# Rows of x held for 20 edge batches in place of 16, three selector buffers, skip pairs every eight batches

## The chip, the cores and the metric

The kernel runs on one core of one Trainium2 chip. The metric is the device time of one execution in microseconds (us); less is better. The engines are named as the profile names them: PE is the matrix engine (PEld its weight loads), DVE the vector engine, ACT the scalar engine, POOL the GpSimd engine, SP the engine that issues plain DMAs. POOL computes next to nothing here: it issues the indirect DMAs that gather rows by index.

## What is computed

One layer of a graph network over 12,500 nodes of 160 channels (64 scalars and 32 vectors of 3) and 400,000 edges that are sorted by destination. Cut to what matters:

```python
h = relu(layernorm(x))                       # per node, 160 channels
y = h @ W_l1 * a / sqrt(..)                  # per node: the scalars with one matrix, the vectors with another
s = h @ W_sc * a / sqrt(..)                  # per node: the skip part
w = silu(edge_attr_4 ... @ fc_W1) @ fc_W2    # per edge: 16 inputs -> 64 -> 192 weights
m = products of w, y[src] and 4 edge values  # per edge: 96 scalars and 96 vectors
z = zeros.at[dst].add(m)                     # sum over the edges of a destination
out = x + C_S * s + C_X * (z @ W_l2) * a     # per node
```

All of it is float32. The length embedding of an edge has 16 values, its attribute 4.

## The kernel before

**Node stage** (lines 393 to 520). The 12,500 nodes are 98 tiles of 128 rows; a step takes two tiles. Each step loads x into `acc`, which later becomes the output, takes mean and variance on DVE (`moments`, `center`), turns the rows on PE (`turn_rows`), maps them with the first weights (`map_rows`) and writes the result y to the DRAM tensor `y_d` (`leave`). The steps run as a software pipeline of eight stages, `q` counts them.

**Edge stage** (lines 537 to 866). The 400,000 edges are 3,125 tiles of 128, and four tiles make a batch: 782 batches, numbered `b`. For each batch

- POOL issues four gathers of 128 rows of y by source index (`gather`, L570), four batches ahead. The first of the four waits for the matmuls of `sums(b - 4)`, by a dependency that is written out by hand.
- PE makes the edge weights from the hidden layer (`weigh`, L603), ACT copies the edge values beside them (L525), and DVE makes a selector (`own` L617, `sel` L619) and the products of weights and rows (`pr`, L530 and L534).
- PE sums the products by destination (`sums`, L633): eight matrix instructions into a window of 32 destinations, held in PSUM. DVE turns a finished window (L639, L640).

A hidden layer for four batches is made every fourth batch: `hidden_pair` at the end of the pass in which `b % 4 == 0`: two matmuls (L583), each into a PSUM buffer of the name `px`, which ACT empties (L588). There are two `px` buffers, and everything small on PE takes them in turn: the hidden layer, the output map of a group (`linear`, L646, emptied by ACT L648), its placing (`add`, L658, emptied by DVE L669), the turning and mapping of the skip part and of the rows of x.

Four windows make a group. A window is 24 tiles wide at the start and gets narrower with the place in the sorted list: 24, 12, 8, 6, 4 and at last 3 tiles, so that a group is 24, 12, 8, 6, 4 or 3 batches. Widths change at batches 96, 192, 312, 408 and 624. `linear`, `add` and `accumulate` of a group run in the second and third batch of the next one.

Two kinds of work are spread over the edge stage.

- **Batches from x.** For XB = 16 batches (b = 19, 35, 51 and so on, every SB = 16th) no row of y is gathered in the edge stage. Their rows of x are fetched during the node stage, while POOL has little else to do (`x_fetch`, L348, four fetches for three steps), and kept in SBUF in `xr`. In the sixteen batches before each is used, its rows are normalized, turned and mapped on the spot: a one-hot matrix (`hot`, DVE L717 and L720; `hot_turn`, PE L728, ACT L730) and matmuls look up scale and mean of the source nodes (`look_up`, PE L740; `pick`, DVE L745 and L746), ACT subtracts the mean (`x_center`, L750), PE turns (`x_turn`, L755 and L756) and maps (`x_map`, L768 and L769).
- **Skip pairs.** The skip part s is made for two node tiles at a time, 49 pairs, one every SK = 10 batches, from batch SS = 16 * XB + 8 = 264 on. Counted from the start of a pair: rows of x are loaded (`skip_load`), centred on DVE in batch 4 (`skip_center`, L686), turned on PE in batch 5 (`skip_turn`, L693 and L694, emptied by ACT L696), mapped in batch 7 (`skip_map`, L703 and L704) and added to the output in the same batch on DVE (`skip_add`, L712).

The order of all instructions on an engine is the order in which the program writes them (`manual_schedule`); the pass of batch b writes `weigh(b + 2)`, `linear` or `add`, the skip and x work, `products(b + 1)`, the adding, `sums(b)`, `gather(b + 4)` and `hidden_pair`.

Of the kernel before, what the change touches and what calls it, by code (L numbers as in the profile page):

```python
# [28 lines left out]
GT = 4  # L29
# [10 lines left out]
EARLY = 8  # L40
SB = 16
LATE = 8
XB = 16
SK = 10
LO = D - P
EPS = 1e-5
C_S = math.sin(math.pi / 8.0)
# [4 lines left out]
def kernel(  # L52
# [36 lines left out]
    NB = (T + GT - 1) // GT  # L89
# [35 lines left out]
    ra, nm = look[:, 0, :], look[:, 1, :]  # L125
    xr = const.tile([P, XB, GT, D], F32, name="xr")
    xi = const.tile([P, XB, GT], I32, name="xi")
    xp = const.tile([P, XB, GT], F32, name="xp")
    xt = const.tile([P, XB, GT], F32, name="xt")
    mv = const.tile([P, NT, 2], F32, name="mv")  # L130
# [177 lines left out]
    def node_dma(g, n, dma):  # L308

        f = min(g + n, N // P) - g  # L310
        if f:
            dma(slice(g * P, (g + f) * P), slice(0, f), P)
        if f < n:
            dma(slice((g + f) * P, N), slice(f, f + 1), N - (g + f) * P)
# [4 lines left out]
    def by_tile(ap):  # L319
        n = ap.shape[0]  # L320
        return ap.rearrange("(t p) c -> p t c", p=min(P, n))
# [8 lines left out]
    def x_batch(u):  # L330

        return SB * (u + 1) + 3

    def x_index():
        t = x_batch(0) * GT
        nc.sync.dma_start(xi, src[:, t:t + XB * SB * GT].rearrange("p (u r) -> p u r", r=SB * GT)[:, :, 0:GT])

    def x_split():

        part = rp.tile([P, XB, GT], I32, name="part")  # L340
        nc.vector.tensor_scalar(part, xi, P - 1, None, ALU.bitwise_and)
# [55 lines left out]
    with (  # L397
        tc.tile_pool(name="ny", bufs=2) as ny,
        tc.tile_pool(name="ns", bufs=4) as ns,
        tc.tile_pool(name="nd", bufs=4) as nd,  # L400
        tc.tile_pool(name="nd_pt", bufs=2, space=PSUM) as nd_pt,
        tc.tile_pool(name="nd_po", bufs=3, space=PSUM) as nd_po,
        tc.tile_pool(name="nd_ph", bufs=2, space=PSUM) as nd_ph,
    ):
        yss, hs, pts, hTs, pos, mapped, sts = ({} for _ in range(7))
        steps = [(g, n, j, min(HN, n - j)) for g, n in groups for j in range(0, n, HN)]

        def moments(q):
            g, n, j, m = steps[q]
            sts[q] = ns.tile([P, HN, 6], F32, name="st")  # L410
            for k in range(m):
                nc.vector.bn_stats(sts[q][:, k, :], acc[:, g + j + k, :])

        def center(q):

            g, n, j, m = steps[q]
            st = sts.pop(q)
            h = nd.tile([P, HN, D], F32, name="h")
            for k in range(m):
                nc.vector.bn_aggr(mv[:, g + j + k, :], st[:, k, :])  # L420
            for k in range(m):
                t = g + j + k
                nc.vector.tensor_scalar(h[:, k, :], acc[:, t, :], mv[:, t, 0:1], 0.0, ALU.subtract, ALU.max)
            hs[q] = h

        def roots(q):
            g, n, j, m = steps[q]
            if j + m == n:
                nc.scalar.activation(ra[:, g:g + n], mv[:, g:g + n, 1], AF.Sqrt, bias=eps)

        def scales(q):

            g, n, j, m = steps[q]
            if j + m == n:
                nc.vector.reciprocal(ra[:, g:g + n], ra[:, g:g + n])
                nc.vector.tensor_mul(ra[:, g:g + n], ra[:, g:g + n], a_sb[:, g:g + n])

        def turn_rows(q):
            m, h = steps[q][3], hs.pop(q)
            pt = nd_pt.tile([P, 2, HN, P], F32, name="pt")  # L440
            for k in range(m):
                nc.tensor.transpose(pt[:, 0, k, :], h[:, k, 0:P], ident)
                nc.tensor.transpose(pt[:, 1, k, :], h[:, k, LO:D], ident)
            pts[q] = pt

        def out_of_psum(q):
            m, pt = steps[q][3], pts.pop(q)
            hT = nd.tile([P, 2, HN, P], F32, name="hT")
            nc.scalar.activation(hT[:, :, :m, :], pt[:, :, :m, :], AF.Copy)
            hTs[q] = hT  # L450

        def map_rows(q):
            m, hT = steps[q][3], hTs.pop(q)
            po = nd_po.tile([P, HN, D], F32, name="po")
            for k in range(m):
                nc.tensor.matmul(po[:, k, 0:M0], hT[:, 0, k, :], wy0, start=True, stop=True)
                mapped[q] = nc.tensor.matmul(po[:, k, M0:], hT[:, 1, k, :], wy1, start=True, stop=True).ins.name  # L457
            pos[q] = po

        def leave(q):  # L460

            g, n, j, m = steps[q]
            if j == 0:
                yss[g] = ny.tile([P, GN, D], F32, name="ys")
            ys, po = yss[g], pos.pop(q)
            for k in range(m):
                nc.scalar.activation(ys[:, j + k, :], po[:, k, :], AF.Copy, scale=ra[:, g + j + k:g + j + k + 1])
            if j + m == n:
                node_dma(g, n, lambda rows, t, p: nc.sync.dma_start(by_tile(y_d[rows, :]), ys[:p, t, :]))
                del yss[g]  # L470


        LEAD = 5
        ready = ns.tile([P, 1], F32, name="ready")
        nc.scalar.activation(ready, eps, AF.Sqrt)
        node_weight_loads()
        edge_zeros()
        for i, (g, n) in enumerate(groups[:LEAD]):
            load_x(g, n)
            if i == 1:  # L480
                nc.sync.dma_start(a_sb, attr)
                x_index()
        last = len(steps) - 1
        more = list(groups[LEAD:])
        loads = edge_weight_loads()
        for q in range(len(steps) + 7):
            if q <= last and steps[q][2] == 0 and more:
                load_x(*more.pop(0))
            for f in range(4 * q // 3, 4 * (q + 1) // 3):
                if f < XB * GT:  # L490
                    x_fetch(f, mapped.get(q - 6))
            if q == 8:
                e4_load(0)
            for load in loads[2 * q - 24:2 * q - 22] if q >= 12 else []:
                load()
            if q == 24:
                for b in range(min(EARLY, NB)):
                    features(b)
            if q == 16:
                rows_of_windows()  # L500
                lowest(0)
            if q == 18:
                pt = nd_ph.tile([MW, P], F32, name="ph")[:windows_in(0), :]
                turn_low(0, pt)
                most(0, pt)
            if q == 22:
                spread(0, nd_ph.tile([P, MW], F32, name="ph")[:, :windows_in(0)])
            for stage, lag in ((scales, 3), (leave, 7), (out_of_psum, 4), (roots, 2), (turn_rows, 3), (map_rows, 5),
                               (moments, 0), (center, 1)):
                if 0 <= q - lag <= last:  # L510
                    stage(q - lag)
            if q == 2:
                node_weights()
            if q == last + 3:
                nc.vector.tensor_scalar(nm, mv[:, :, 0], -1.0, None, ALU.mult)
                x_split()
                edge_weights()
                relate(rp, 0)
        assert 12 + len(loads) // 2 <= last and 3 * XB * GT <= 4 * (last + 8) and x_batch(XB) <= NB
    before.close()  # L520


# [12 lines left out]
                                 wt[:, :n, 96 * x + M0:96 * (x + 1)].unsqueeze(2).to_broadcast([P, n, 3, M1]), y1)  # L535

    with (
        tc.tile_pool(name="selp", bufs=4) as selp,
        tc.tile_pool(name="prod", bufs=3) as prod,
        tc.tile_pool(name="xq", bufs=1) as xq,  # L540
        tc.tile_pool(name="sp", bufs=2) as sp,
# [131 lines left out]
        def skip_load(u):  # L673

            t, m = HN * u, min(HN, NT - HN * u)
            xs = sp.tile([P, HN, D], F32, name="xs")
            if t + m == NT and N % P:
                nc.vector.memset(xs[:, m - 1, :], 0.0)
            node_dma(t, m, lambda rows, k, p: nc.sync.dma_start(xs[:p, k, :], by_tile(x[rows, :])))
            xss[u] = xs, t, m  # L680
# [94 lines left out]
            nc.vector.tensor_tensor(part, part, vals[u][:, :, 0:1].to_broadcast([P, GT, 4]), ALU.mult)  # L775

        NU = (NT + HN - 1) // HN
        skips = {4: skip_center, 5: skip_turn, 7: skip_map, 8: lambda u: skip_load(u + 1) if u + 1 < NU else None}
        SS = SB * XB + 8
        xs_of = {x_batch(u) for u in range(XB)}  # L780

# [12 lines left out]
        for b in range(NB):  # L794
# [4 lines left out]
            q, r = divmod(b, KB)  # L799
# [4 lines left out]
            u, v = divmod(b, SB)  # L804
            su, sv = divmod(b - SS, SK)
            if b + 2 < NB:
# [28 lines left out]
                products(b + 1)  # L835
            if g and k == K - 1:
                accumulate(g - 1)
            if sv == 7 and 0 <= su < NU:
                skip_add(su)
            if picked is not None:  # L840
                pick(u, HN * (v == 6), *picked)
# [17 lines left out]
            if b % 4 == 0 and b + 4 < NB:  # L859
                hidden_pair((b + 4) // 2)  # L860
        assert SS + NU * SK <= first_of[GE] + K and NQ > 1
        for h in ([NG - 2] if NG > 1 else []) + [NG - 1]:
# [160 lines left out]
```

## Time and profile before

| | |
|---|---|
| three runs | 4700.06, 4708.81 and 4720.77 us, median 4708.81 |
| profiled execution | 4710.64 us, of which its instructions span 4708.8 |
| before the span's start and after its end | 1.8 us |
| first gather of y (end of the node stage) | at 115.6 us |
| first and last `own` (L617) of the 782 batches | 118.7 and 4694.6 us |
| busy: PE, DVE, POOL, ACT | 3891.7, 2736.7, 2968.3, 581.6 us |
| mean granted clock of PE | 0.906 of full |

How to read it: a group of instructions is given by its line, engine, operation and tiles, then the number of instructions, a bar, their busy time and the mean of one in ns, a second bar and the idle time of the engine just before them, with what ended most of that. A wait is put down to the engine whose semaphore came last. `remote` stands for a release that the profile can't name, `issue` for time in which the engine waited for nothing that it shows. Ends of matmuls are modelled. An indirect DMA on POOL is busy only while it is issued; its rows land later.

### The profile page before, as it was taken

The numbers are of one execution on the slowest core, as the hardware profiler recorded it, in microseconds if no ns is written. First come the engines' busy times: TensorE is split into PE (matmuls) and PEld (weight loads), VectorE is DVE, ScalarE is ACT, GpSimd is POOL, SyncE is SP. The second block draws the span as 40 slices with busy tenths as digits, with TensorE's granted clock in tenths as the row PEclk, the third lists the DMA queues.
The fourth block names the chain that finished last, engine by engine and source line by source line (L and its number), as shares of the span: only waits on it lengthen the run. The fifth ranks groups of instructions, "written<-read, shape, count | busy, mean of one in ns | idle before, by whom it ended". The sixth has DMA issues, their size and how long they took to land.

```text
span 4708.8 us, 46910 instructions
## 1 busy us (share of the span) xinstructions
PE 3891.7 (83%) x14078; PEld 2542.2 (54%) x14078; DVE 2736.7 (58%) x6877; ACT 581.6 (12%) x1845; POOL 2968.3 (63%) x3145
## 2 busy tenths in 40 slices
PE   7788888888788787887888888888888888888888
PEld 6455555555555455555555555555555555555555
DVE  5555555555555555555555656556556666666665
ACT  5111111111111101101110101111011111111100
POOL 5666666666666666666666666666666666666665
PEclk8889999999999998988888989998989998998889
DMA  7222222222222222222222222222222222222224
GB/s 192 69 63 65 66 66 65 66 67 64 60 64 67 66 69 67 67 66 67 70 68 62 65 63 67 66 68 63 63 66 65 68 64 63 65 64 67 59 62 117
DMA packets 262471, 328.58 MB, mean 70 GB/s; under 512 B 82888, under 2 KB 212216, under 8 KB 262216
## 3 DMA queue, kind: packets, MB, share of 16 engines
q0 software_dynamic: 150128, 256.23, 20.5%
q1 hardware_dynamic: 111590, 69.02, 5.2%
q8 instruction: 116, 1.90, 0.2%
q14 instruction: 139, 1.14, 0.1%
q10 hardware_dynamic: 498, 0.30, 0.0%
HBM read 307.67 MB, written 17.61 MB: 69 GB/s over the span
## 4 chain that ended last, share of the span: by engine, by line
PE 66%; another core or an unknown queue 15%; issue 7%; DVE 7%; ACT 2%; ACTq 1%; POOL 0%; DMA 0%; DVEq 0%; SPq 0%; POOLq 0%
PE pz L633 31%; PE pw L603 19%; PE px L646 6%; PE px L583 3%; DVE pr L534 2%; PE px L658 2%; DVE pr L530 1%; ACT hT L588 1%; ACTq L525 1%; DVE za L640 1%; DVE za L639 1%; PE po L457 1%; PE px L704 1%; POOL yg L570 0%
## 5 line engine op out<-in xcount | busy, mean ns | idle before, releaser
L570 POOL DMA_INDIRECT yg<-y_d,src_q x3061 | 2901.9, 948 | 1681.5 <-issue 795.2
L633 PE MATMUL pz<-pr,sel 128*128 128x320 f32 x6250 | 1950.3, 457 | 17.6 <-DVE za L640 15.2
L633 PEld LDWEIGHTS pz<-pr,sel 128*128 128x128 f32 x6250 | 1243.5, 204 | 542.6 <-issue 94.9
L603 PE MATMUL pw<-w,hT 128*128 128x384 f32 x3126 | 1233.8, 519 | 208.7 <-DVE pr L534 135.6
L603 PEld LDWEIGHTS pw<-w,hT 128*128 128x128 f32 x3126 | 590.3, 198 | 734.3 <-issue 375.5
L639 DVE STREAM_TRANSPOSE za<-pz 128x160 f32<-128x160 f32 x598 | 206.5, 345 | 1298.9 <-PE pz L633 551.3
L534 DVE TENSOR_TENSOR pr<-pw,yg 128x384 f32<-128x384 f32 x1532 | 773.5, 546 | 0.0
L530 DVE TENSOR_TENSOR pr<-pw,yg 128x512 f32<-128x512 f32 x766 | 523.2, 683 | 126.8 <-DMA yg<-y_d,src_q 118.3
L646 PE MATMUL px<-wo,za 128*128 128x160 f32 x1500 | 320.2, 376 | 294.4 <-ACT hT L588 198.2
L619 DVE TENSOR_TENSOR sel<-own,pw 128x512 f32<-128x512 f32 x782 | 536.9, 687 | 28.1 <-issue 1.2
L646 PEld LDWEIGHTS px<-wo,za 128*128 128x128 f32 x1500 | 290.2, 246 | 364.7 <-ACT hT L588 226.5
L525 ACT ACTIVATE pw<-ev 128x20 f32<-128x20 f32 x782 | 149.6, 191 | 2624.1 <-PE pw L603 970.4
L588 ACT ACTIVATE hT<-px 128x512 f32<-128x512 f32 x391 | 218.5, 595 | 968.9 <-remote 648.9
L583 PE MATMUL px<-xe,w 32*128 32x512 f32 x782 | 268.9, 658 | 66.2 <-ACT os L648 38.8
L617 DVE TENSOR_TENSOR own<-iota,pw 128x128 f32<-128x128 f32 x782 | 200.0, 256 | 177.1 <-ACT pw L525 133.8
L640 DVE STREAM_TRANSPOSE za<-pz 32x160 f32<-32x160 f32 x598 | 202.1, 338 | 20.5
L658 PE MATMUL px<-os,place 128*128 128x160 f32 x600 | 122.6, 332 | 79.0 <-ACT os L648 75.8
L669 DVE SCALAR_TENSOR_TENSOR acc<-px,a_sb,acc 128x160 f32 x300 | 113.9, 380 | 113.2 <-PE px L658 70.8
L658 PEld LDWEIGHTS px<-os,place 128*128 128x128 f32 x600 | 107.0, 211 | 131.8 <-ACT os L648 91.2
L583 PEld LDWEIGHTS px<-xe,w 32*128 32x128 f32 x782 | 70.9, 187 | 176.8 <-issue 95.7
L648 ACT ACTIVATE os<-px 128x160 f32<-128x160 f32 x150 | 45.3, 302 | 359.8 <-remote 168.4
L712 DVE SCALAR_TENSOR_TENSOR acc<-px,look,acc 128x160 f32<-128x160 f32 x98 | 32.9, 377 | 95.1 <-PE pz L633 39.7
(129 smaller groups left out, 1423.7 us busy)
## 6 DMA issues: line engine op xcount, KB each, us to landing
yg<-y_d,src_q POOLq DMA_INDIRECT x3061
xe<-in_e SPq DMA_DIRECT2D x784, 32.0 KB
xs<-in_x SPq DMA_DIRECT2D x48, 160.0 KB
acc<-in_x SPq DMA_DIRECT2D x11, 640.0 KB
y_d<-ys SPq DMA_DIRECT2D x11, 640.0 KB
out<-acc SPq DMA_DIRECT2D x11, 640.0 KB
raw<-in_e SPq DMA_DIRECT2D x32, 192.0 KB
src_q<-in_src SPq DMA_DIRECT2D x32, 48.0 KB
```

Of the source, the lines that this page charges most:

```text
L530: nc.vector.tensor_mul(pr[:, :n, :].rearrange("p t (x u) -> p t x u", x=2)[:, :, :, 0:M0], wt[:, :n, 0:NW].rearrange("p t (x u) -> p t x u ...
L534: nc.vector.tensor_mul(pr[:, :n, D * x + M0:D * (x + 1)].rearrange("p t (c u) -> p t c u", c=3), wt[:, :n, 96 * x + M0:96 * (x + 1)].unsqu ...
L570: fetch = nc.gpsimd.indirect_dma_start(out=yg[:, slot(t), :], out_offset=None, in_=y_d, in_offset=bass.IndirectOffsetOnAxis(ap=ev4[t // BL ...
L583: nc.tensor.matmul(ph, w1[r, :], xe[r, :], start=True, stop=True)
L588: nc.scalar.activation(hT, ph, AF.Silu, scale=1.0 / math.sqrt(FC_IN))
L603: nc.tensor.matmul(pw[:, 2 * k:2 * k + m, 0:NW], hT[:, o:o + P], w2[:, :m, :], start=True, stop=True)
L619: nc.vector.tensor_tensor(sel, own[:, :n, :].unsqueeze(2).to_broadcast([P, n, 4, WN]), wt[:, :n, NW:NW + 4].unsqueeze(3).to_broadcast([P, ...
L633: mm = nc.tensor.matmul(pz[:, 0:PC], sel[:, slot(t), :, :], pr[:, slot(t), :], start=o == 0, stop=last)
L639: nc.vector.transpose(zT[g][:, :, at_w], pz[:, D:PC].rearrange("p (k u) -> p k u", k=ZK))
L640: nc.vector.transpose(zT[g][0:32, :, at_w], pz[0:32, 0:D].rearrange("p (k u) -> p k u", k=ZK))
L646: nc.tensor.matmul(po[:m, :], za[:, k, :m], wo[:, k, :], start=k == 0, stop=k == ZK - 1)
L658: nc.tensor.matmul(ps[:, h, :], place[:m, h, :], os[:m, :], start=True, stop=True)
```

## The change

Three constants of the work spread over the edge stage change, and one pool.

- XB goes from 16 to 20. Twenty batches (b = 19 to 323) take their rows from x, so 64 fetches in the node stage become 80 and 3061 gathers become 3045. The fetches stand five to three node steps, and each still waits for the map of six steps before.
- The pool `selp`, which holds `own` and `sel`, has three buffers in place of four. `xr` grows by four times 4 x 160 floats for each partition.
- Skip pairs start at batch SS = 328 in place of 264, follow each other every 8 batches in place of 10, and centre, turn, map and load one batch earlier within a pair (3, 4, 6, 7 in place of 4, 5, 7, 8). The last of the 49 pairs begins at batch 712 in place of 744.

The diff:

```diff
-XB = 16
-SK = 10
+XB = 20
+SK = 8
...
-            for f in range(4 * q // 3, 4 * (q + 1) // 3):
+            for f in range(5 * q // 3, 5 * (q + 1) // 3):
                 if f < XB * GT:
                     x_fetch(f, mapped.get(q - 6))
...
-        tc.tile_pool(name="selp", bufs=4) as selp,
+        tc.tile_pool(name="selp", bufs=3) as selp,
...
-        skips = {4: skip_center, 5: skip_turn, 7: skip_map, 8: lambda u: skip_load(u + 1) if u + 1 < NU else None}
+        skips = {3: skip_center, 4: skip_turn, 6: skip_map, 7: lambda u: skip_load(u + 1) if u + 1 < NU else None}
...
-            if sv == 7 and 0 <= su < NU:
+            if sv == 6 and 0 <= su < NU:
                 skip_add(su)
```

Where a skip pair stands among the batches also changes. Since 264 and 328 are multiples of four, and 10 is not, a pair before was turned at b % 4 = 1 and mapped at 3, and the next one turned at 3 and mapped at 1, by turns. Now every pair is centred at b % 4 = 3, turned at 0 and mapped at 2.

PE's order around one skip pair of the stretch with windows of four tiles, before, from `sums(466)` on. L693 and L694 are the pair's turning, L646 and L658 `linear` and `add`, L583 the hidden layer, L178 and L187 small work on the next window starts:

```order
L633 MATMUL pz<-pr,sel 128x320 x4
L603 MATMUL pw<-w_94,hT 128x2x192 x2
L633 MATMUL pz<-pr,sel 128x320 x4
L583 MATMUL px<-xe,w_93 128x512 x2
L603 MATMUL pw<-w_94,hT 128x2x192 x2
L646 MATMUL px<-wo,za 128x160 x5
L693 MATMUL px<-ident,sh 128x128
L694 MATMUL px<-ident,sh 128x128
L693 MATMUL px<-ident,sh 128x128
L694 MATMUL px<-ident,sh 128x128
L187 MATMUL px<-ident,high 128x24
L633 MATMUL pz<-pr,sel 128x320 x4
```

The same place now, from `weigh(470)` on:

```order
L603 MATMUL pw<-w_94,hT 128x2x192 x2
L693 MATMUL px<-ident,sh 128x128
L694 MATMUL px<-ident,sh 128x128
L693 MATMUL px<-ident,sh 128x128
L694 MATMUL px<-ident,sh 128x128
L633 MATMUL pz<-pr,sel 128x320 x4
L583 MATMUL px<-xe,w_93 128x512 x2
L603 MATMUL pw<-w_94,hT 128x2x192 x2
L646 MATMUL px<-wo,za 128x160 x5
L187 MATMUL px<-ident,high 128x24
L633 MATMUL pz<-pr,sel 128x320 x4
```

The turning stood behind the hidden layer and behind `linear`; now it stands ahead of the sums and of the hidden layer, and takes a `px` buffer before the hidden layer takes both.

POOL's order, whole but for its start:

```order
 L262 MEMSET wor 128x800
 L264 MEMSET acc 128x160
-L348 DMA xr<-in_x,xi 128x160 x64
-L570 DMA yg<-y_d,src_q 128x160 x3061
+L348 DMA xr<-in_x,xi 128x160 x80
+L570 DMA yg<-y_d,src_q 128x160 x3045
 L876 TENSOR_LOAD far_i
```

Sixteen indirect DMAs move from the edge stage to the node stage, and nothing else of POOL's moves.

More of the change, by code (lines that the diff above doesn't have):

```diff
@@ L518 @@
                 relate(rp, 0)
-        assert 12 + len(loads) // 2 <= last and 3 * XB * GT <= 4 * (last + 8) and x_batch(XB) <= NB
+        assert 12 + len(loads) // 2 <= last and 3 * XB * GT <= 5 * (last + 8) and x_batch(XB) <= NB
     before.close()
```

## The prediction

> **What bounds the kernel now.** I read the page first, the engines' shares and the costliest groups.
>
> ```profile
> PE 3891.7 (83%) x14078; PEld 2542.2 (54%) x14078; DVE 2736.7 (58%) x6877; ACT 581.6 (12%) x1845; POOL 2968.3 (63%) x3145
> L570 POOL DMA_INDIRECT yg<-y_d,src_q x3061 | 2901.9, 948 | 1681.5 <-issue 795.2
> ```
>
> No engine is full. PE at 83% looks like the bound, but ends of matmuls are modelled and overlap. POOL is the one to look at: a gather is busy for 948 ns, yet the waits of POOL show a second cost that always comes with it.
>
> ```profile
> POOL yg L570 <- issue: 795.2, 2541, 4.6
> POOL yg L570 <- PE pz L633: 372.5, 149, 7.2
> POOL yg L570 <- remote: 314.1, 131, 3.7
> POOL yg L570 <- PE pw L603: 85.0, 66, 4.9
> ```
>
> 795.2 us over 2541 waits is 0.31 us each: the gap between two gathers in which POOL waits for nothing. So a gather takes 0.95 + 0.30 = 1.25 us of POOL, 3061 of them 3826 us, and four, a batch's worth, 5.0. The rest, 372.5 + 314.1 + 85.0 = 772 us in 346 waits, 2.2 us each, are stops in which POOL has used up its lead of four batches. The edge stage is thus POOL's queue plus its stops. The timeline shows what a stop is: POOL, then PE, then ACT in one of them, each row with start, duration and, in brackets, the idle time before it.
>
> ```profile
> 2511.18 0.94 POOL L570 DMA_INDIRECT yg<-y_d,src_q  x1 [0.30 <-issue]
> 2512.43 0.94 POOL L570 DMA_INDIRECT yg<-y_d,src_q  x1 [0.30 <-issue]
> 2515.77 0.94 POOL L570 DMA_INDIRECT yg<-y_d,src_q  x1 [2.39 <-remote]
> ...
> 2509.68 1.13 PE L583 MATMUL px<-xe,w 32*128 32x512 f32 x4
> 2511.64 1.56 PE L603 MATMUL pw<-w,hT 128*128 128x384 f32 x4 [0.84 <-DVE pr L534]
> 2516.22 1.80 PE L646 MATMUL px<-wo,za 128*128 128x160 f32 x10 [3.02 <-ACT hT L588]
> ...
> 2515.57 1.09 ACT L588 ACTIVATE hT<-px 128x512 f32<-128x512 f32 x2 [5.44 <-remote]
> ```
>
> The hidden pair fills both `px` buffers. The next user of `px`, here `linear`, needs one back and sits in PE's queue ahead of `sums(b + 1)`. ACT gets the hidden layer 4.8 us after PE's rows end (2509.68 + 1.13 against 2515.57), and POOL has run dry by then. So a small `px` user close behind, or ahead of, a hidden pair makes a stop.
>
> How long a batch takes by stretch is read from the rows of L617 (one for each batch) and of L570 in equal windows of time: four rows of the one, then three of the other. The first stretch is b = 192 to 267 (x batches), the second 268 to 311 (skip pairs; windows eight tiles wide in both), the third 624 to 753 (skip pairs, width 3), the last 754 to 780 (neither).
>
> ```profile
> 1176.10:1612.10 436.00, 19.76 (x76) 0.93 0.24 64
> 1612.10:1868.90 256.80, 11.58 (x44) 0.89 0.25 67
> 3740.30:4536.40 796.10, 32.25 (x130) 0.90 0.24 64
> 4536.40:4694.60 158.20, 6.66 (x27) 0.90 0.36 104
> ...
> 1176.10:1612.10 436.00, 273.81 (x289) 0.93 0.24 64
> 1612.10:1868.90 256.80, 165.95 (x176) 0.89 0.25 67
> 3740.30:4536.40 796.10, 493.26 (x521) 0.90 0.24 64
> ```
>
> A batch takes 5.74, 5.84, 6.12 and 5.86 us. Less 1.25 us for each gather, stops are 0.98 us a batch with x batches (436.0 - 361.3, over 76), 0.84 with skip pairs (256.8 - 220.0, over 44), 1.11 in the third.
>
> **The change part by part.** *Gathers.* Sixteen fewer in the edge stage: 16 x 1.25 = 20.0 us off POOL's queue.
>
> *The work that four x batches bring.* Their groups, with means of one:
>
> ```profile
> L740 PE MATMUL px<-look,sT 128*128 128x196 f32 x128 | 28.0, 344 | 2.4 <-ACT sT L730 2.1 <-issue 0.3
> L769 PE MATMUL px<-wy,sT 128*128 128x96 f32 x128 | 28.6, 308 | 0.0
> L768 PE MATMUL px<-wy,sT 128*128 128x64 f32 x128 | 24.4, 275 | 17.8 <-ACT hT L588 13.4 <-issue 4.4
> L755 PE MATMUL px<-ident,xr 128*128 128x128 f32 x64 | 20.0, 330 | 48.6 <-ACT hT L588 37.0 <-issue 8.5 <-ACT sT L758 3.0
> L756 PE MATMUL px<-ident,xr 128*128 128x128 f32 x64 | 19.4, 322 | 0.0
> L728 PE MATMUL px<-ident,oh 128*128 128x128 f32 x64 | 9.6, 273 | 0.0
> ```
>
> A sixteenth of the six is 8.1 us of busy PE, overlap taken off. DVE's and ACT's shares, a few us, lie beside engines that are 58% and 12% busy. What decides is not this but the stops: one `x_turn` and one `x_map` in sixteen batches stand at b % 4 = 1, right behind a hidden pair; 37.0 of L755's 48.6 us of idle time ended with ACT's hidden layer. From the stretches of equal width, x batches cost 0.98 - 0.84 = 0.14 us a batch more in stops if the skip pairs of the second stretch are free, 2.3 us for each x batch; and (0.14 + 0.27) x 16 = 6.6 if a skip pair costs what the last two stretches say (6.12 - 5.86 = 0.27 a batch, 2.7 a pair; an upper bound, since the last stretch is short and POOL runs out within it). Against 5.0 us saved, one x batch is worth between a gain of 2.7 and a loss of 1.6 us, four between -11 and +6. I take the middle, **-2 us**: the saving of 20 and a return of 18.
>
> *Skip pairs.* All 49 stay; none of them stands at b % 4 = 1 any more, where before each pair had one part, the turning or the mapping. That part came after `linear`, on the second `px` buffer, so it waited for the second hidden activation too (0.5 of the 1.09 us of L588 above), and its own 0.44 us (turning) or some 0.9 (mapping; below) stood before `sums(b + 1)` in the one pass of four that POOL waits for.
>
> ```profile
> 2503.44 0.27 PE L693 MATMUL px<-ident,sh 128*128 128x128 f32 x1
> 2503.99 2.32 PE L633 MATMUL pz<-pr,sel 128*128 128x320 f32 x8
> ...
> 2517.81 0.53 PE L703 MATMUL px<-ws,sT 128*128 128x64 f32 x2
> 2518.61 0.58 PE L703 MATMUL px<-ws,sT 128*128 128x64 f32 x2
> 2519.61 0.30 PE L187 MATMUL px<-ident,high 24*128 24x24 f32 x1
> ```
>
> The turning (L693, L694) runs from 2503.44 to 2503.88, the mapping, in the stretch above at half clock, from 2517.81 to 2519.61, so about 0.9 at full. Taken out of that pass, 0.5 + 0.65 = 1.15 us a pair, 56 us for 49, is the most. The least is nothing: 0.44 us is now ahead of `sums(b)` at b % 4 = 0, and 0.9 plus `skip_add` at 2, beside `add`. The cover there is POOL's lead, refilled by then; without it the 1.3 us a pair is back. I take a third, **-18 us**, because the stop itself stays wherever `linear` makes it: always in the 216 batches of width 4, which get 27 of the 49 pairs.
>
> *Selector buffers*: **0**. `sel(b + 1)` with three buffers waits for `sums(b - 2)`. It needs `weigh(b + 1)` anyway, and that stands behind `sums(b - 2)` in PE's order. If that cover were gone, `own` and `sel` (0.26 + 0.69 us) would come late.
>
> *Node stage.* Sixteen more fetches of 1.25 us are 20 us of POOL. POOL's rows there:
>
> ```profile
> 7.79 1.03 POOL L348 DMA_INDIRECT xr<-in_x,xi  x1 [1.76 <-DMA xi<-in_src]
> 102.99 0.95 POOL L348 DMA_INDIRECT xr<-in_x,xi  x1 [0.30 <-issue]
> 115.56 0.95 POOL L570 DMA_INDIRECT yg<-y_d,src_q  x1 [11.62 <-DMA xe<-in_e]
> ...
> 0.00:50.00 50.00, 33.72 (x217) 31.82 (x218) 28.64 (x154) 21.74 (x55) 32.63 (x49) 0.89 0.89 239
> ```
>
> 80 fetches without a pause end at 7.8 + 80 x 1.25 = 108, before the first gather, which waits for y and not for POOL. But the DMA engines are 89% busy in the first 50 us at 239 GB/s, and 16 fetches of 82 KB are 1.3 MB: 0 to 5.5 us. I take **+2**, because later they have room.
>
> *Sum*, against the profiled execution: 4710.6 - 20 + 18 - 18 + 0 + 2 = **4693 us**; the runs' median lies 1.8 below that execution.
>
> **The rivals.** *The turning blocks the hidden pair* (slower). The turning at b % 4 = 0 takes one `px` buffer; the first half of the hidden pair gets the other, and the second half must wait until ACT has copied the turning. The trace has this place with `linear` in it, where windows are three tiles wide:
>
> ```profile
> 3767.49 1.52 PE L646 MATMUL px<-wo,za 128*128 128x160 f32 x10
> 3768.85 2.32 PE L633 MATMUL pz<-pr,sel 128*128 128x320 f32 x8
> 3771.10 1.12 PE L583 MATMUL px<-xe,w 32*128 32x512 f32 x2
> 3776.48 2.07 PE L583 MATMUL px<-xe,w 32*128 32x512 f32 x2 [4.25 <-ACT os L648]
> ...
> 3776.12 0.30 ACT L648 ACTIVATE os<-px 128x160 f32<-128x160 f32 x1 [7.55 <-remote]
> ```
>
> The second half waited 4.25 us, for an ACT copy that began 7.1 us after PE's rows of `linear` end. For it: the same buffers in the same order. Against it: ACT takes a turning at once where sums follow (2503.44: L696 is not among the long waits), and there 2.3 us of sums lie in between. If it holds, the 27 pairs in width 4 only exchange one stop for another, the 22 others get a stop of 4.25 us, half of which POOL's lead can take: 22 x 4.25 / 2 = 47, the skip gain of 18 is gone: 4710.6 - 2 + 47 + 2 = **4757 us**. It decides from a mean wait of about 1 us at L583's second half.
>
> *PE's clock.* [...] The row of `linear` at 2516.22 stretches to 1.80 us from 1.52 after 3.02 us of waiting, and the second half of L583 above takes 2.07 where the first takes 1.12: PE runs at half clock after a long wait. [...]
>
> *Gathers come off in full* (faster). POOL's queue gets 20 us shorter and the x work hides, as a stop that is there anyway takes it; the skip pairs give 18 to 56, say 30: 4710.6 - 20 - 30 + 2 = **4662 us**. For it: POOL is the queue that never waits long. Against it: the stretches, 0.98 against 0.84.
>
> *It does nothing*: one stop in four batches stays, whatever else is put there: 4710.6 + 2 = **4712 us**.
>
> **How the numbers follow.** The forecast gets 0.38, with 4675 to 4712 as its own range; blocked hidden pairs 0.34, full saving 0.20, nothing 0.08. The range of 8 in 10 takes in most of both sides: 4650 to 4768. About 0.5%, 24 us, is what a measurement of this kernel can tell from no change, so faster is below 4687 and slower above 4734. Faster: 0.17 of the forecast's 0.38, 0.20 of the full saving: 0.37. Slower: 0.29 of the blocked pairs' 0.34 and 0.01 of the forecast: 0.30. Same: 0.33.
>
> **What would show it.** POOL's gathers: 3045 at 0.95 us, and 16 more fetches. If the gathers' 20 us are given back, POOL's stops (the three waits above) grow by about as much as the gathers shrink; in b = 268 to 327 a batch takes about what it takes in b = 192 to 267. If the skip step is right, batches between 328 and 719 are faster by 0.05 us each. If L583 waits for ACT's L696 by tens of us in all, the blocked pairs are it, and the forecast is wrong. A first gather later than 118 us makes the node term wrong.

## The result, and the profile after

The changed kernel takes 4686.35 us (median of 7 runs, 4676.10 to 4693.68) against 4708.81 us (7 runs, 4700.06 to 4720.77): a ratio of 0.996, 95% interval 0.9942 to 0.9977. The prediction said 4693. Its total came out right, but by luck: two of its parts were off by about 20 us each, in opposite directions, as the profile shows. The profiled execution took 4693.68 us.

First the page, its row of the engines and the groups of POOL and of the hidden layer. The last number pair of a group is the idle time ahead of it and what ended most of it.

```profile
PE 3913.0 (83%) x14222; PEld 2543.0 (54%) x14222; DVE 2747.7 (59%) x6905; ACT 598.7 (13%) x1881; POOL 2973.1 (63%) x3145
L570 POOL DMA_INDIRECT yg<-y_d,src_q x3045 | 2891.6, 950 | 1649.9 <-issue 794.0
L348 POOL DMA_INDIRECT xr<-in_x,xi x80 | 76.3, 954 | 43.4 <-issue 18.9
L583 PE MATMUL px<-xe,w 32*128 32x512 f32 x782 | 292.1, 665 | 114.7 <-ACT os L648 42.4
```

Sixteen indirect DMAs have moved as planned, and POOL still issues 3145 instructions in all. Its idle time ahead of gathers fell from 1681.5 to 1649.9 us: the stops did not take back what the gathers gave. The hidden layer's matmuls (L583), though, now wait 114.7 us; before it was this.

```profile
L583 PE MATMUL px<-xe,w 32*128 32x512 f32 x782 | 268.9, 658 | 66.2 <-ACT os L648 38.8
```

Next the node stage: the 196 matrix instructions of its last map (L457) with the start of the first and the last, then POOL's fetches, with the idle time before each in brackets. Of each pair of fences the first is of before, the second of after.

```profile
L457 PE MATMUL po<-wy,hT x196: 274/302/476, 11.2 to 108.5; 128*128 128x96 f32 x196
...
57.63 0.94 POOL L348 DMA_INDIRECT xr<-in_x,xi  x1 [1.10 <-PE pt L443]
...
63.98 1.01 POOL L348 DMA_INDIRECT xr<-in_x,xi  x1 [1.59 <-remote]
...
70.03 0.95 POOL L348 DMA_INDIRECT xr<-in_x,xi  x1 [1.29 <-PE po L457]
```

```profile
L457 PE MATMUL po<-wy,hT x196: 275/302/476, 11.1 to 131.6; 128*128 128x96 f32 x196
...
61.62 0.95 POOL L348 DMA_INDIRECT xr<-in_x,xi  x1 [1.48 <-remote]
...
69.08 0.95 POOL L348 DMA_INDIRECT xr<-in_x,xi  x1 [1.50 <-PE pt L443]
...
137.05 0.95 POOL L570 DMA_INDIRECT yg<-y_d,src_q  x1 [11.36 <-DMA xe<-in_e]
```

Three node steps hold a run of four fetches and a pause: 63.98 - 57.63 = 6.35 and 6.05 us. Now they hold five and a pause: 69.08 - 61.62 = 7.46 us, one fetch of 1.25 us more. The last map starts 23.1 us later. The first gather moved from 115.6 to 137.1 us, by 21.5 us: the 20 us of POOL that left the edge stage all come back in the node stage.

So the gain lies in the edge stage. The windows view gives DVE's `own` (L617) by stretch: from and to, length, busy time, number of batches, granted clock, DMA share, GB/s. The stretches are b = 268 to 327, 328 to 407, 408 to 623 and 624 to 719, first of before, then of after.

```profile
1612.06:1965.36 353.30, 15.62 (x60) 0.90 0.25 66
1965.36:2427.37 462.01, 20.16 (x80) 0.90 0.26 69
2427.37:3740.28 1312.91, 53.34 (x216) 0.91 0.24 65
3740.28:4328.10 587.82, 23.86 (x96) 0.91 0.24 65
```

```profile
1638.66:1979.90 341.24, 15.48 (x60) 0.91 0.23 63
1979.90:2443.91 464.01, 20.16 (x80) 0.91 0.26 69
2443.91:3725.37 1281.46, 53.56 (x216) 0.92 0.25 68
3725.37:4305.93 580.56, 23.89 (x96) 0.91 0.24 65
```

The stretch that turned from skip pairs to x batches is 12.1 us shorter, the 216 batches with windows four tiles wide 31.5 us, the next 7.3 us. From the first `own` to the last the edge stage went from 4575.9 to 4535.0 us, by -41. How far such a difference of two single executions can be trusted: batches 96 to 191, which the change touches only through the selector buffers, took 525.4 us before and 535.2 after.

What changed in those 216 batches is in PE's waits inside that window: what waited, for whom, us in total, times, longest. First before, then after.

```profile
PE px L646 <- ACT hT L588: 122.6, 32, 4.5
PE px L646 <- issue: 78.9, 16, 6.5
```

```profile
PE px L646 <- ACT hT L588: 63.1, 22, 3.8
PE px L583 <- issue: 24.1, 12, 2.9
PE px L583 <- ACT sT L696: 16.4, 9, 2.1
PE px L646 <- issue: 14.1, 5, 3.9
```

`linear` behind the hidden pair waited 201.5 us and now waits 77.2. A new wait has come in its place, 40.5 us of L583, which is the second half of the hidden pair behind the turning: the blocked pair of the rivals, 40.5 / 54 = 0.75 us for each of the 54 pairs of this stretch.

### The profile page after: what moved, and what is told of

The parts are those of the page before. It is cut to its first block, busy times and chain, and to the rows that moved or that the text cites. A ratio compares the mean times of both kernels' runs of the same rounds, so it can differ in the third digit from the quotient of the medians.

```text
span 4691.7 us, 47207 instructions
## 1 busy us (share of the span) xinstructions
PE 3913.0 (83%) x14222; PEld 2543.0 (54%) x14222; DVE 2747.7 (59%) x6905; ACT 598.7 (13%) x1881; POOL 2973.1 (63%) x3145
## 4 chain that ended last, share of the span: by engine, by line
PE 64%; another core or an unknown queue 15%; issue 7%; DVE 7%; ACT 2%; POOL 1%; ACTq 1%; DVEq 0%; DMA 0%; POOLq 0%
PE pz L633 30%; PE pw L603 19%; PE px L646 5%; PE px L583 4%; DVE pr L534 2%; PE px L658 2%; DVE pr L530 1%; POOL yg L570 1%; ACT hT L588 1%; DVE za L639 1%; DVE za L640 1%; PE px L704 1%; PE px L740 1%; ACTq L525 1%
## 5 line engine op out<-in xcount | busy, mean ns | idle before, releaser
L570 POOL DMA_INDIRECT yg<-y_d,src_q x3045 | 2891.6, 950 | 1649.9 <-issue 794.0
L633 PE MATMUL pz<-pr,sel 128*128 128x320 f32 x6250 | 1930.4, 454 | 10.2 <-DVE za L640 8.5
L633 PEld LDWEIGHTS pz<-pr,sel 128*128 128x128 f32 x6250 | 1227.5, 202 | 523.0 <-issue 90.0
L603 PE MATMUL pw<-w,hT 128*128 128x384 f32 x3126 | 1252.9, 526 | 227.6 <-DVE pr L534 138.3
L603 PEld LDWEIGHTS pw<-w,hT 128*128 128x128 f32 x3126 | 594.8, 200 | 766.1 <-issue 418.8
L619 DVE TENSOR_TENSOR sel<-own,pw 128x512 f32<-128x512 f32 x782 | 537.0, 687 | 28.5 <-issue 1.1
L525 ACT ACTIVATE pw<-ev 128x20 f32<-128x20 f32 x782 | 149.5, 191 | 2589.1 <-PE pw L603 1146.7
L646 PE MATMUL px<-wo,za 128*128 128x160 f32 x1500 | 298.6, 358 | 170.3 <-ACT hT L588 147.8
L646 PEld LDWEIGHTS px<-wo,za 128*128 128x128 f32 x1500 | 278.6, 236 | 238.7 <-ACT hT L588 177.8
L583 PE MATMUL px<-xe,w 32*128 32x512 f32 x782 | 292.1, 665 | 114.7 <-ACT os L648 42.4
L617 DVE TENSOR_TENSOR own<-iota,pw 128x128 f32<-128x128 f32 x782 | 200.2, 256 | 165.4 <-ACT pw L525 112.3
L658 PE MATMUL px<-os,place 128*128 128x160 f32 x600 | 123.8, 334 | 118.3 <-ACT os L648 107.8
L583 PEld LDWEIGHTS px<-xe,w 32*128 32x128 f32 x782 | 77.3, 189 | 241.5 <-issue 132.8
L658 PEld LDWEIGHTS px<-os,place 128*128 128x128 f32 x600 | 105.7, 211 | 176.1 <-ACT os L648 130.3
L348 POOL DMA_INDIRECT xr<-in_x,xi x80 | 76.3, 954 | 43.4 <-issue 18.9
```

Source lines behind the costliest of these rows:

```text
L570: fetch = nc.gpsimd.indirect_dma_start(out=yg[:, slot(t), :], out_offset=None, in_=y_d, in_offset=bass.IndirectOffsetOnAxis(ap=ev4[t // BL ...
L583: nc.tensor.matmul(ph, w1[r, :], xe[r, :], start=True, stop=True)
L603: nc.tensor.matmul(pw[:, 2 * k:2 * k + m, 0:NW], hT[:, o:o + P], w2[:, :m, :], start=True, stop=True)
L619: nc.vector.tensor_tensor(sel, own[:, :n, :].unsqueeze(2).to_broadcast([P, n, 4, WN]), wt[:, :n, NW:NW + 4].unsqueeze(3).to_broadcast([P, ...
L633: mm = nc.tensor.matmul(pz[:, 0:PC], sel[:, slot(t), :, :], pr[:, slot(t), :], start=o == 0, stop=last)
L646: nc.tensor.matmul(po[:m, :], za[:, k, :m], wo[:, k, :], start=k == 0, stop=k == ZK - 1)
```

## The experiments

The runs fell on two chips, and what follows needs that told. The one, here the second chip, takes 3956 us for the kernel before, with a granted clock of 0.989; the other, the third, takes 4727.93 us (27 runs, 4705.10 to 4744.34). The runs of the result are called the first chip: by its 4709 us it is not the second; whether it is the third at another time is not recorded.

**The second chip.** Four kernels.

*The skip places alone.* Before, with

```diff
-SK = 10
+SK = 8
-        skips = {4: skip_center, 5: skip_turn, 7: skip_map, 8: ...
+        skips = {3: skip_center, 4: skip_turn, 6: skip_map, 7: ...
-            if sv == 7 and 0 <= su < NU:
+            if sv == 6 and 0 <= su < NU:
```

> XB stays 16, four fetches for three steps, selectors in four buffers; only the skip pairs are moved to every eight batches with turning at b % 4 = 0 and mapping at 2 (they start at 264). Theory A (the gain comes from where the skip pairs stand; x batches only move POOL's 20 us from the edge stage into the node stage): about 4687 us, 18 to 26 us less than before, first gather still near 116 us, and the 216 batches of width 4 shorter by about 30 us. Theory B (the gain comes from the four more x batches, as POOL's queue gets shorter): within 8 us of before, 4701 to 4717 us.

Measured: 3956.56 us against 3956.06, ratio 1.0 (0.9991 to 1.0009).

*The x batches alone.* The changed kernel, with the skip parts at 4, 5 and 7 of a pair (so turned at b % 4 = 1 in every pair and mapped at 3; the kernel before alternates):

```diff
-        skips = {3: skip_center, 4: skip_turn, 6: skip_map, 7: ...
+        skips = {4: skip_center, 5: skip_turn, 7: skip_map, 6: ...
-            if sv == 6 and 0 <= su < NU:
+            if sv == 7 and 0 <= su < NU:
```

> The changed kernel (20 x batches, five fetches for three steps, three selector buffers, skip pairs every eight batches), but with the parts of a skip pair where they were within it: centred, turned and mapped at 4, 5 and 7, so that all 49 pairs are turned at b % 4 = 1, behind the hidden pair (the next load moves to 6). Theory A: the gain of 22 us is gone, 4705 us or more, since every pair now has the place that half of them had; first gather near 137 us. Theory B: 4680 to 4693 us, as the changed kernel.

Measured: 3951.39 us, ratio 0.9986 (0.9977 to 0.9995).

*Fetches that don't wait for the map of six steps before.*

```diff
-                    x_fetch(f, mapped.get(q - 6))
+                    x_fetch(f, None)
```

> The changed kernel, in which the fetches of x in the node stage don't wait for the maps of six steps before. Theory M (PE's completions reach the other engines only when POOL pauses in its indirect DMAs, so that the node stage goes at the pace of the fetches): POOL issues 80 fetches in one go from 8 to 108 us, the steps hardly advance meanwhile, and the first gather comes well after 137 us, near 160 or more. Rival (the node stage was slower only because the fetches wait for the maps and the transfers compete): the first gather comes at 110 to 125 us and the kernel gains some 15 us.

Measured: 3950.3 us, one run, first gather at 109.1 us.

*The hidden pair one pass earlier*, so that it stands at the end of b % 4 = 3 and `linear` of the widths 4 and more, but for 6, is two passes behind it; the skip parts one batch later, so that no turning stands ahead of it:

```diff
-        skips = {3: skip_center, 4: skip_turn, 6: ...
+        skips = {4: skip_center, 5: skip_turn, 6: ...
...
+        hidden_pair(2)
...
-            if b % 4 == 0 and b + 4 < NB:
-                hidden_pair((b + 4) // 2)
+            if b % 4 == 3 and b + 5 < NB:
+                hidden_pair((b + 5) // 2)
```

> The changed kernel with the hidden pair made one batch earlier, at the end of the pass with b % 4 = 3, and the skip pairs centred, turned and mapped at 4, 5 and 6, so that with windows of four tiles no small user of px stands right behind the hidden pair. Theory S (a stop is made by a px user that is queued behind the hidden pair before its activation): the stop in each four batches of width 4 goes, those 216 batches take 5.0 to 5.5 us each in place of 5.93, and the kernel ends at 4450 to 4600 us. Rival (POOL stops for another reason, such as its lead of four batches, and the stop comes wherever the hidden pair is): within 1% of the changed kernel, 4640 to 4730 us.

Measured: 3948.86 us, ratio 0.9982 (0.9972 to 0.9991).

None of the four could tell the theories apart, because this chip has no stops. POOL's longest waits and the group of gathers in the run with the x batches alone:

```profile
POOL yg L570 <- issue: 678.1, 2226, 0.3
POOL yg L570 <- PE pw L603: 104.8, 344, 0.3
POOL yg L570 <- DVE acc L669: 20.7, 68, 0.3
...
L570 POOL DMA_INDIRECT yg<-y_d,src_q x3045 | 2887.4, 948 | 931.9 <-issue 678.1
```

The waits shown are 0.3 us each, whatever they are put down to: 931.9 over 3045 gathers is 0.306 us, the bare gap. POOL issues without a stop, a batch takes 1.25 us for each gather, and where skip work stands decides nothing, as e1's ratio of 1.0 says. What is left of the change is four x batches, worth 5 us of 3956.

The node stage there shows where the rest of their 20 us went. The last map starts at the same time with 64 fetches (the skip places alone) and with 80 (the x batches alone):

```profile
L457 PE MATMUL po<-wy,hT x196: 274/302/475, 11.5 to 92.7; 128*128 128x96 f32 x196
```

```profile
L457 PE MATMUL po<-wy,hT x196: 274/302/475, 11.2 to 92.4; 128*128 128x96 f32 x196
```

The node steps do not feel the fetches; only POOL itself is busy with them longer than y needs, so the first gather moves from 99.4 to 108.7 us. On the first chip the same steps slowed by 23.1 us though they use nothing that the fetches bring.

**The third chip.** It has the stops: the same four questions again, with the changed kernel itself.

> The changed kernel itself, beside the runs to come. If POOL has stops (the kernel before near 4700 us): ratio 0.993 to 0.998 as measured first, first gather near 137 us against 116, edge stage (first to last selector) some 40 us shorter. If POOL has none (before near 3956 us): the skip places weigh nothing, the edge stage is shorter by the 16 gathers, 20 us, the node stage longer by 9, ratio 0.997 to 0.999; the theory that the move pays only where there are stops says 1.000.

Measured: 4749.05 us (10 runs, 4730.84 to 4761.04), ratio 1.0037 (1.0017 to 1.0056). On this chip the change makes the kernel slower, by 21 us, which the expectation did not have. First gather at 139.1 us.

> Only the skip pairs change (XB stays 16, four selector buffers, four fetches for three node steps). Theory S (what the change gained came from the skip places): with POOL's stops, edge stage 25 to 45 us shorter, nothing in the node stage, ratio 0.990 to 0.995, better than the whole change. Theory X (it came from the gathers): ratio 0.999 to 1.001. Without stops both say 1.000, as before.

The same kernel as e1. Measured: 4772.33 us (6 runs), ratio 1.01 (1.0072 to 1.0129): 44 us slower, where theory S had it 25 to 45 us faster in the edge stage and theory X no change. Both fall. First gather at 116.5 us, so the loss lies in the edge stage.

> Only the x batches change (XB 20, five fetches for three steps, skip parts at 4, 5, 6 and 7 of a pair, every eight batches, so that turning is again at b % 4 = 1, behind the hidden pair). Theory S: with POOL's stops, the node stage gives 21 us and the edge stage takes back at most that, ratio 0.998 to 1.004, worse than the whole change by 20 to 40 us. Theory X: as good as the whole change, within 8 us. Without stops both say 0.9986, as before, and within 3 us of the whole change.

The same kernel as e2. Measured: 4753.55 us (10 runs), ratio 1.0053 (1.0038 to 1.0069): 26 us slower, and within 5 us of the whole change. First gather at 138.8 us. The node stage's 22 us over e7's, whose node stage is that of the kernel before, come near all of it. Theory X had the whole change met within 8 us, as it was, and theory S had this kernel 20 to 40 us above it; but X fell with the run before. The two parts alone cost 44 and 26 us, and together 21: they do not add up, and these runs give no price for either of them.

> The changed kernel with the hidden pair written one pass earlier (end of b % 4 = 3) and the skip parts one batch later. Theory S in its wider form (a stop is made by the small user of px that stands next to a hidden pair): with POOL's stops in width 4 linear stands two passes behind it, so POOL's idle time beyond the 0.3 us gaps falls by a fifth or more and the time is 50 us or more below the whole change. If stops come from lateness of PE's signals wherever a pass waits for them: no more than 20 us either way. Without stops: 2 us below the whole change at most.

The same kernel as e5. Measured: 4700.88 us (10 runs, 4669.87 to 4737.31), ratio 0.9962 (0.9931 to 0.9993), and 48 us below the whole change on the same chip, where the wider form of theory S said 50 or more and the lateness theory no more than 20. POOL's idle time ahead of gathers fell only from 1712.4 to 1654.9 us against the changed kernel; taking 0.305 us off for each of 3045 gathers, from 784 to 726, 7% and not the fifth that was expected. The time came near theory S, the idle time did not. In the 216 batches of width 4 `linear` and the hidden layer are gone from the long waits, and `add` (L658) and `weigh` (L603) stand there instead:

```profile
PE px L658 <- ACT os L648: 71.2, 26, 4.8
PE pw L603 <- DVE pr L534: 63.4, 34, 3.3
PE pw L603 <- issue: 37.4, 21, 3.1
```

What the blocked pair costs is read from the waits of the 216 batches of width 4 again: the changed kernel, the skip places alone, and the x batches alone.

```profile
PE px L646 <- ACT hT L588: 59.4, 19, 4.1
PE px L583 <- issue: 36.4, 12, 3.8
PE px L583 <- ACT sT L696: 36.4, 8, 5.3
```

```profile
PE px L583 <- ACT sT L696: 66.9, 15, 5.3
PE px L646 <- ACT hT L588: 57.9, 18, 5.2
...
PE px L583 <- issue: 21.7, 8, 3.6
```

```profile
PE px L646 <- ACT hT L588: 123.8, 33, 4.8
PE pw L603 <- DVE pr L534: 50.5, 30, 5.4
PE px L646 <- issue: 23.0, 8, 5.2
```

Turned behind `linear` (the x batches alone), L583 is not among the waits listed, which go down to 3.5 us, and `linear` waits 146.8 us. Turned ahead of the hidden pair, `linear` waits about half of that, and L583 waits 72.8 us in the changed kernel and 88.6 with the skip places alone. One wait has taken the other's place. In the profiled executions these 216 batches took 1332.5 us with the turning ahead (the changed kernel) and 1299.5 with it behind (the x batches alone), while batches 328 to 407 and 624 to 719 took 469.8 and 583.7 against 480.3 and 603.6. These are single executions again, but on this chip width 4 lost where on the first chip it gained. One such pair of the changed kernel on the timeline, PE, then ACT, then POOL:

```profile
2581.82 0.27 PE L693 MATMUL px<-ident,sh 128*128 128x128 f32 x1
2582.14 0.27 PE L694 MATMUL px<-ident,sh 128*128 128x128 f32 x1
2582.25 2.32 PE L633 MATMUL pz<-pr,sel 128*128 128x320 f32 x8
2584.50 1.12 PE L583 MATMUL px<-xe,w 32*128 32x512 f32 x2
2590.63 2.07 PE L583 MATMUL px<-xe,w 32*128 32x512 f32 x2 [5.01 <-ACT sT L696]
...
2589.98 0.60 ACT L696 ACTIVATE sT<-px 128x512 f32<-128x512 f32 x1 [2.60 <-remote]
...
2586.66 0.95 POOL L570 DMA_INDIRECT yg<-y_d,src_q  x1 [0.30 <-issue]
2590.31 0.95 POOL L570 DMA_INDIRECT yg<-y_d,src_q  x1 [2.70 <-remote]
```

The turning is over at 2582.41 by PE's rows. ACT, which empties it, begins at 2589.98, 7.6 us later and 2.4 us after POOL's last gather ended (2587.61). But for one copy of 0.19 us (L525, at 2587.18) it was not busy: it waited for releases. Two things meet in this stop, then: a matmul that needs a `px` buffer back, and a completion of PE that reaches ACT late. The same place on the second chip has the first and lacks the second:

```profile
2215.32 0.27 PE L694 MATMUL px<-ident,sh 128*128 128x128 f32 x1
2215.43 2.32 PE L633 MATMUL pz<-pr,sel 128*128 128x320 f32 x8
2217.68 1.13 PE L583 MATMUL px<-xe,w 32*128 32x512 f32 x4
...
2215.63 0.60 ACT L696 ACTIVATE sT<-px 128x512 f32<-128x512 f32 x1 [0.20 <-PE px L694]
```

This is the skip places alone, again turned ahead of the hidden pair. ACT begins 0.04 us after the turning ends (2215.59), both halves of the hidden pair run on without a wait, and POOL gathers on.

**Four more kernels** were to try the blocked pair (theory P) and the node stage (N and M) on a chip with stops. They ran on the second chip, without them.

*Skip pairs centred at b % 4 = 1, turned at 2, mapped at 3*, the changed kernel otherwise:

```diff
-        skips = {3: skip_center, 4: skip_turn, 6: skip_map, 7: ...
+        skips = {5: skip_center, 6: skip_turn, 7: skip_map, 0: lambda u: skip_load(u) if u else None}
-            if sv == 6 and 0 <= su < NU:
+            if sv == 7 and 0 <= su < NU:
```

> The changed kernel with every skip pair centred at b % 4 = 1, turned at 2 and mapped and added at 3 (loaded at the pair's first batch): no skip work stands in the passes before or behind a hidden pair. Theory P (the turning at b % 4 = 0 blocks the second half of the hidden pair, and that takes back what the skip places gained): with POOL's stops, the second half of L583 waits 0 us in batches 408 to 623 (73 us in the changed kernel on the chip of the runs before), and the time is 20 to 50 us below the changed kernel's on the same chip. Rival L (stops come with late signals after each hidden pair, whatever stands beside it): the waits move to linear, and the time is within 15 us of the changed kernel's. Without stops (the kernel before near 3956): as the changed kernel, 0.998 to 1.000.

Measured: 3952.54 us against 3956.79, ratio 0.9988 (0.9979 to 0.9997).

*18 x batches, four fetches for three steps*, the changed kernel otherwise:

```diff
-XB = 20
+XB = 18
-            for f in range(5 * q // 3, 5 * (q + 1) // 3):
+            for f in range(4 * q // 3, 4 * (q + 1) // 3):
```

> The changed kernel with 18 x batches and four fetches for three node steps as before; skip pairs keep their residues (from batch 296 on). Theory N (the node stage runs in step with POOL's fetches, so its length goes by the fetches in three steps, not by their total): with stops first gather at 115 to 118 us against 137, edge stage 10 us longer by its eight gathers, time 8 to 14 us below the changed kernel's. Rival T (the length goes by the total of fetches): 72 x 1.25 = 90 against 80 and 100, first gather near 126, time the same within 3 us. Without stops: first gather near 100 to 104, time 0 to 6 us below the kernel before.

Measured: 3953.36 us, ratio 0.999 (0.9981 to 0.9999), first gather at 101.3 us.

*The same with the hidden pair one pass earlier*, as in e5.

> The same with the hidden pair one pass earlier and the skip parts one batch later. If both gains add, with stops 8 to 14 us below the kernel with the earlier hidden pair and 20 x batches, whose ratio was 0.996: ratio 0.992 to 0.995. If the edge stage's stops fill what the node stage gives: ratio 0.996 or more. Without stops: 5 to 10 us below the kernel before.

Measured: 3951.34 us, ratio 0.9987 (0.9978 to 0.9996), first gather at 99.7 us.

*Unpaced fetches again*, in ten runs; the same kernel as e3.

> The changed kernel without the fetches' wait for the map of six node steps before. Theory M (this dependency ties node steps and fetches together): with stops POOL issues 80 fetches without a pause until about 108 us, the node steps run free beside it, first gather at 112 to 120 us against 137, and the time is about 20 us below the changed kernel's. Rival F (PE's completions reach the others late while POOL issues indirect DMAs back to back, whatever POOL waits for): the node steps get no faster, first gather at 137 us or later. Without stops: no difference, as before (109.1 against 108.7).

Measured: 3949.98 us (10 runs), ratio 0.9984 (0.9975 to 0.9993), first gather at 109.0 us against 108.7 with the wait.

All four meet what was expected of a chip without stops, and so decide nothing between their theories. That turning at 2 would free the hidden pair, and that four fetches would win the node stage's 21 us back on a chip with stops, was not shown. What they add: 64, 72 and 80 fetches give a first gather at 99.4, 101.3 and 108.7 us, so without stops the eight fetches beyond 72 push it back by 7.4 us, and the eight before them by 1.9.

## Why the prediction was right, and where not

- **What bounds the kernel: right.** The edge stage is POOL's queue plus its stops. The second chip shows it from the other side: 3045 gathers at 1.25 us without stops, and 3951 us. The 772 us of stops in the prediction are only the three longest kinds of wait, each with its gap of 0.3 us; what lies beyond the gaps is 1681.5 - 3061 x 0.305 = 748 us.
- **16 gathers, -20: right.** 3045 at 950 ns, the gap unchanged.
- **The x work gives 18 back: within what the runs allow, not settled.** In b = 268 to 327 a batch takes 341.24 / 60 = 5.69 us, near the x stretch of before (5.74), as the prediction's mark had it. The stretch lost 20 us of gathers and six skip pairs, and is 12.1 us shorter: the x work took 8 us back if those pairs cost nothing there, and 24 if each cost the 2.7 us of the prediction's upper bound; two executions differ by 10 us in batches 96 to 191 already. The other mark, stops that grow by what the gathers shrink, was not met: POOL's idle time fell by 31.6 us, but the skip pairs' gain is in that too.
- **Skip pairs, -18: the mark met on the first chip, the place wrong, the cause not shown.** Batches 328 to 719 took 2362.7 us and take 2326.1 (the last three rows of each fence added), 0.093 us less for each, where 0.05 was the mark. In width 4 `linear` waits 124 us less and L583 40.5 more. But the prediction took only a third of the 56 us because it left the stop of width 4 in place, and there the stretch got 31.5 of the 36.6 us shorter. Nor is it shown that the skip places did it: on the third chip moving them alone went the other way, by 44 us, and the changed kernel and the one with the x batches alone, which differ only in them, lie within 5 us.
- **Node stage, +2: this step failed, and it is what the total hides.** It set the DMA engines' room against 80 x 1.25 us that end before the first gather, and concluded that the fetches lie in time which POOL has to spare. On this chip the node steps keep pace with the fetches, 1.25 us for each fetch and a pause of 1.2 for each three steps, and the term is +21.5. Its own mark (a first gather later than 118 us) caught it. The rows for it were in the trace of before: four fetches and a pause in every three steps.
- **Selector buffers, 0: nothing against it.** `sel` (L619) waited 28.1 us before and 28.5 after. No run changed them alone.
- **The sum.** By the `own` rows it is +21.8 for the node stage and -40.9 for the edge stage, -19 in all (-17 between the profiled executions, as what follows the last `own` is 2 us longer), where the prediction had +2 and -20. Two errors of about 20 us, in opposite directions, left a total within 7 us of the median: that is luck.
- **The rival of the blocked pair** was in play and not decisive on the first chip, and its wait is there on the third, where the skip places cost time. The prediction let it decide from a mean wait of about 1 us at L583's second half. In the 54 pairs of width 4 that mean is 0.75 us on the first chip, where the change won, and 72.8 / 54 = 1.35 on the third, where its edge stage won next to nothing: 21 us slower in all, with a node stage 22.6 us longer (139.1 against the 116.5 of e7). With the skip places alone it is 1.64. That the loss of 44 us is near the 47 that the rival was priced at does not bear out the price: it was made of 22 pairs outside width 4, each with a stop of 4.25 us, 93.5 in all, and there L583 waits only 22.8 us for L696 (89.7 in the whole run, 66.9 in width 4). On PE's clock there are rows too: the second half in the timeline above takes 2.07 us after a wait of 5.01, where the first took 1.12. In the like pair of before (L583 at 3771.10 and 3776.48, 1.12 us and, after a wait of 4.25, 2.07) the granted clock is 1.00 over the first half and 0.50 over the second, and it is 0.50 over the mapping that the prediction put at half clock (2517.81 to 2519.61). What the clock adds to the cost of a stop no run shows; the sum that gave 4693 has no term for it.

Open: why the edge stage of one and the same changed kernel takes 4535 us on the first chip and 4593 on the third, while the kernel before differs by 19 us between them; and why PE's completions arrive at once on the second chip (99 of 100 of ACT's copies start within 0.09 us of them) and not in the other runs (39 and 40% start more than 1 us after them in the two that were counted). The traces show that it is so; no run here separates a chip from the condition it was in.

## What to carry to other kernels

Work that fills an engine's spare time is free only if the steps beside it do not slow with it (the 16 fetches put the first gather off by 21.5 us on the first chip): look in the trace for the pace of those steps before calling the time spare. When two buffers are shared by a pair of matmuls and by small users, a small user that is moved from behind the pair to ahead of it can move the wait as well (on the third chip, in width 4, `linear` waits 76.2 us in place of 146.8, and L583 now waits 72.8); of the four kernels on the third chip, the one with the pair moved away from its neighbours alone beat the kernel before (0.9962; on the second chip 0.9982, where the x batches alone gave 0.9986). And a gain of half a per cent that rests on such waits can have the other sign on another chip or another day (0.996 and 1.0037 for this change), so it is worth measuring more than once.

## What the runs showed of the hardware

The same program takes 3956 us on one chip and 4709 to 4728 in the other runs, though a gather is busy for 946 to 950 ns and `sel` for 687 on each. What differs in the traces is when PE's completions reach the others. ACT's copy of the edge values (L525) starts more than 1 us after the modelled end of the last `weigh` matmul ahead of it in 39% of the 782 batches before on the first chip (75th percentile 3.2 us), in 40% with the skip places alone on the third, and in none with the same kernel on the second, where 99 of 100 start within 0.09 us. In the node stage, ACT's copy of the turned rows (L449) starts a median of 1.9 us after the turning (its last L442) before on the first chip, 2.8 with the change, and 0.17 on the second with 64 fetches as with 80.

In the two stops shown, on the first and the third chip, ACT's late start comes 2.2 and 2.4 us after POOL's last gather ended. That POOL's indirect DMAs hold such releases back fits this, and fits node steps that keep pace with fetches they do not use, but it was only argued: no run took the gathers away. By themselves the gathers do not explain it. On the second chip POOL gathers without a stop and nothing is late; and before, on the first chip, 296 of the 474 copies that are not late start in the middle of a row of back-to-back gathers (more than 2.5 us after its start), as do 88 of the 308 late ones.
